# First layer of a four-layer network: input also channels first, norms moved to ScalarE, slots of some side work moved

## The chip, the cores and the metric

The kernel runs on one core of a Trainium2 chip. A core has five engines with a queue of instructions each: TensorE (PE in the profile, with its weight loads shown apart as PEld), VectorE (DVE), ScalarE (ACT), GpSimd (POOL) and SyncE (SP), which here issues the DMA transfers. The engines run side by side and wait for each other by semaphores; each takes its own instructions strictly in order. The metric is the device time of one execution in microseconds (us); lower is better. Times of one execution with the hardware profiler on give the trace.

## The reference, cut to what matters

Four layers follow each other on `x` of shape (4, 64, 64, 128). Only the first is touched. It is a two-dimensional selective-scan block with a group norm before it and a residual around it:

```
g   = group_norm(x)                                # 32 groups of 4 channels, per image
xh, z = split(g @ in_proj.T); z = silu(z)          # 256 channels each
xc  = silu(depthwise_conv3x3(xh) + conv_b)         # SAME padding
for k in 4 directions:                             # rows, columns, and both reversed
    dts, B, C = split(xs[k] @ x_proj[k])           # 8, 16 and 16 columns
    delta = softplus(dts @ dt_proj[k] + bias)
    h[t]  = exp(delta[t] * A) * h[t-1] + delta[t] * xs[t] * B[t]    # 16 states, 4096 steps
    y[k]  = sum over states of C[t] * h[t]  + D * xs
y   = layer_norm(y[0] + y[1] + y[2] + y[3])        # over 256 channels, per pixel
x   = x + (y * z) @ out_proj.T
```

The other three layers (a Fourier block, a neural-operator attention and a neighbourhood attention) read the result and are the same in both kernels.

## The kernel before, in words

`layer0` (from L83) goes through 128 *units*: 4 images x 4 directions x 8 chunks of 512 pixels (`units`, L512). A unit has 16 *slots*, one per state `n` of the scan, and a slot numbers the whole layer's time: `slot = 16 * i + n`. In text, "unit 5 of image 1" is the sixth unit of the second image.

In each slot: GpSimd multiplies `dB = du * B` for 1024 elements (L689); ScalarE makes two `dA = exp(delta * A)` (L694) into PSUM; VectorE runs two scans of 512 steps (L695); TensorE transposes 8 blocks of `h` from some slots earlier into the single PSUM tile `pt` (L542); ScalarE copies `pt` to `hT` (L552), which frees `pt`; TensorE multiplies the last slot's `hT` with the C weights into two `yT` banks (L577). Fixed extra steps lie in fixed slots by the table `TABLE`: the projection `x` in slot 6, its two copies in 7, and the delta steps between slots 7 and 12. The sum of a direction leaves the `yT` banks in slots 5 and 7 (L593).

The order on TensorE, ScalarE, VectorE and GpSimd is written out by hand (`tc.manual_schedule`). Work that does not belong to the scan is put between by *sides*: generators that yield one letter per piece, the kind of the piece. A kind may run only in the slots that `SIDE` lists, a piece keeps others off for `SPACE` slots, and `Side.due` spreads the pieces over the image. What a piece starts is finished by `later(place, f, slots=k)`: it is queued for `k` slots on, at a place in the slot (`dve` before the scans, `act0` after the first `dA`, `act1` after the second, `act2` after the copy `hT`). Two sides matter here:

- `before(b)` (L305) prepares image `b` while image `b - 1` is scanned. For each of 8 chunks it loads pixels-first input (`xs`, L313), transposes it on TensorE and takes statistics on VectorE (L318). After `group_scale` it loads the input again (`xt`), transposes it again (L336), and VectorE writes the scaled chunk from PSUM into the padded tile `xn` of 10 rows by 66 columns, with one or two more single rows for the neighbours (L635 with the tile `xn`). Then the two gate products `zp` (L177) with their SiLU, and two convolutions of nine taps each (L159), one tap in a slot, with theirs. SiLU is Exp, Ln, Exp on ScalarE and a product on VectorE (`silu`, L347).
- `after(b)` (L375) finishes image `b` while image `b + 1` is scanned: loads of `y` and `z`, aggregation, ln and exp for the factor `nb` (L396), the layer norm by VectorE (`normed`, L423, four instructions), transposes `pg` (L404), scale and shift on ScalarE into `yg`, the gating product on GpSimd (L412, kind `g`, only in slot 7 and only for images 0 to 2), the product with `w_out` (L417) in the PSUM tile `spare`, of which there is one, and the residual (L426). For image 3 it starts in that image's last quarter and takes each band as its last direction is done.

The first image's preparation (`opening`, L187) leaves two chunks' convolutions to a side `rest` (L297).

Of the kernel before, what the change touches and what calls it, by code (L numbers as in the profile page):

```python
# [17 lines left out]
P = 128  # L18
# [64 lines left out]
def layer0(sh, A, x_in, x_out, scr, ahead):  # L83
# [7 lines left out]
    with ExitStack() as ctx:  # L91
# [60 lines left out]
        def conv(xn, s, bank):  # L152

            for t in range(9):
                yield "c"
                if t == 0:
                    pm = bank("cv")
                dy, dx = divmod(t, 3)
                nc.tensor.matmul(  # L159
                    pm,  # L160
                    lhsT=taps[:, s, t, :],
                    rhs=xn[:, dy : dy + 8, dx : dx + 64],
                    start=(t == 0),
                    stop=(t == 8),
                )
            return pm
# [6 lines left out]
        def gates(b, c, v, bank, later, es=(None, None)):  # L173
            for s in range(2):
# [3 lines left out]
                silu(zp, 0.0, 0.0, scr(f"z{b % 3}")[s, :, c * CH : (c + 1) * CH], later, (("act1", 1), ("act2", 1), 2), es[s])  # L178
# [6 lines left out]
        def opening(bank, steps):  # L185
# [82 lines left out]
            for c in range(DENSE + 1):  # L268
# [9 lines left out]
                if c < DENSE:  # L278
                    for _ in gates(0, c, xg[:, 8 * c : 8 * c + 8], bank, soon):
                        pass  # L280
                    for _ in conv(xn, 0, lambda name: pm):
                        pass
# [15 lines left out]
        def rest(tiles, bank, later):  # L298

            for c, xn in enumerate(tiles, DENSE):  # L300
                for s in range(2):
                    pm = yield from conv(xn, s, bank)
                    grown(0, c, s, pm, later)

        def before(b, bank, later):  # L305
# [4 lines left out]
            for c in range(NCH):  # L310
                yield "l"
                t = tmp.tile([P, 4, DM], F32, name="xs", tag="t2", bufs=4)
                nc.sync.dma_start(t, tiles(x_in(b)[c * CH : (c + 1) * CH, :]))  # L313
                yield "m"
                pt = bank("gn_ps")
                for q in range(4):
                    nc.tensor.transpose(pt[:, q * P : (q + 1) * P], t[:, q, :], sh.ident)
                later("dve", lambda c=c, pt=pt: nc.vector.bn_stats(st[:, c, :], pt))  # L318
            yield "m"
            s_, o_ = sh.group_scale(st, psm, small, "m", exp_rstd)  # L320
            xn, ahead = None, rows()
            nc.gpsimd.memset(ahead[:, 0, :], 0.0)
            for c in range(NCH + 1):
                behind, xn = xn, ahead
                if c < NCH:
                    yield "l"
                    t = tmp.tile([P, 4, DM], F32, name="xt", tag="t2", bufs=4)
                    nc.sync.dma_start(t, tiles(x_in(b)[c * CH : (c + 1) * CH, :]))
                    if c < NCH - 1:
                        ahead = rows()  # L330
                    else:
                        nc.gpsimd.memset(xn[:, 9, :], 0.0)
                    yield "x"
                    pt = bank("x_ps")
                    for q in range(4):
                        nc.tensor.transpose(pt[:, q * P : (q + 1) * P], t[:, q, :], sh.ident)  # L336
                    grid = pt.rearrange("p (h w) -> p h w", w=64)
                    parts = [(xn[:, 1:9, 1:65], grid)]
                    if c > 0:
                        parts.append((behind[:, 9:10, 1:65], grid[:, 0:1]))  # L340
                    if c < NCH - 1:
                        parts.append((ahead[:, 0:1, 1:65], grid[:, 7:8]))
                    for dst, src in parts:
                        later("dve", nc.vector.tensor_scalar, dst, src, s_, o_, ALU.mult, ALU.add)
                    yield from gates(b, c, xn[:, 1:9, 1:65], bank, later)
                if c == 0:
                    continue  # L347
                for s in range(2):
                    pm = yield from conv(behind, s, bank)
                    grown(b, c - 1, s, pm, later)  # L350
# [24 lines left out]
        def after(b, st, later, bands):  # L375

            for c in bands:
# [15 lines left out]
                yield "n"  # L393

                nb = spare("nb")[:, 0:4]
                nc.scalar.activation(nb, rs, AF.Exp, scale=-0.5)  # L396
                for q in range(4):
                    later("dve", normed, y[:, q, :], mv[:, q, 0:1], nb[:, q : q + 1])
# [11 lines left out]
                if b < NB - 1:  # L410
                    yield "g"
                nc.gpsimd.tensor_tensor(yg, yg, z, ALU.mult)  # L412
                yield "m"
                op = spare("op").rearrange("p (q d) -> p q d", q=4)
# [140 lines left out]
        def products(G, q, hT):  # L555
# [67 lines left out]
            z={0, 1, 2, 3, 4, 11, 12, 13, 14, 15},  # L623
            c={11},
            g={7},
            f=(),
            l=(),
        )
        SPACE = dict(m=1, x=1, n=1, z=2, c=3, g=0)
# [11 lines left out]
        def flush_all():  # L641
            for at in range(slot, slot + 6):
# [3 lines left out]
        with tc.manual_schedule(engines=order):  # L646
# [3 lines left out]
            sides.append(Side(rest(left, spare, later), 18 * len(left), 0, 2 * NS * len(left)))  # L650
            for i, (b, k, c) in enumerate(units):
                if i % per == 0:
                    ln_st = small.tile([P, NJ, 1, 6], F32, name="ln_st")
                    first = len(left) if b == 0 else 0
                    if b + 1 < NB:
                        sides.insert(len(sides) if b == 0 else 0, Side(before(b + 1, spare, later), 17 + 8 * 22, NS * (i + first), (28 - first) * NS))
# [20 lines left out]
                for n in range(NS):  # L677
# [55 lines left out]
                    for d in inside or [d for d in sides if free and n in SIDE[d.need] and d.due(slot)][:1]:  # L733
# [3 lines left out]
                    for d in sides:  # L737
                        if d.need in ("f", "l") and d.due(slot):
# [38 lines left out]
class Side:  # L777


    def __init__(self, pieces, count, first, slots, loads=()):  # L780
        self.pieces, self.count, self.first, self.slots, self.loads = pieces, count, first, slots, list(loads)
        self.done, self.run, self.free_at = 0, 0, first
# [1298 lines left out]
def lay_out(i):  # L2081
# [96 lines left out]
    a["x"] = i["x"].reshape(4, NT, DM)  # L2178
    return {k: np.ascontiguousarray(v) for k, v in a.items()}
# [16 lines left out]
```

## Time and profile before

| | us |
|---|---|
| median of 3 runs (7655.22 to 7660.92) | 7658.74 |
| the profiled execution | 7655.2 |
| its span, first to last instruction | 7653.4 |
| scans of image 0 (111.9 to 1487.1) | 1375.2 |
| scans of image 1 (to 2871.1) | 1384.0 |
| scans of image 2 (to 4254.7) | 1383.6 |
| scans of image 3 (to 5611.5) | 1356.8 |
| the rest, mainly layers 1 to 3 | 2041.9 |

A line of a group in the profile names the line of the kernel, the engine, the operation, the tiles written and read, the shapes and the count; after the bar come the busy time, the mean duration in ns, and the idle time of the engine just before these instructions with what ended it. A line of a timeline has the start, the time from start to end of the merged instructions, the engine and the operation, and in brackets the wait before. An engine's instructions overlap a little at their ends, so the distance from start to start is some 0.09 us shorter than a duration. The helper `activation` and some others record a common line number, L635, so these are told apart by their tiles.

### The profile page before, as it was taken

How to read it: one execution, taken by the hardware profiler on the slowest of the kernel's cores; microseconds unless marked ns; L12 is line 12 of the kernel's file. 1: busy time of each engine (PE TensorE's matmuls, PEld its weight loads, DVE VectorE, ACT ScalarE, POOL GpSimd, SP SyncE). 2: the span in 40 equal slices, each digit the busy share in tenths (PEclk: the TensorE clock that was granted, in tenths of full speed). 3: DMA queues.
4: the chain of work that ended last, by engine and by line, in shares of the span. 5: the costliest groups of instructions: out<-in, count | busy, mean ns of one | idle time of the engine just before them, and what ended most of it. 6: DMA issues, size and time to landing. Idle time of an engine off the chain costs nothing.

```text
span 7653.4 us, 140855 instructions
## 1 busy us (share of the span) xinstructions
PE 6305.5 (82%) x52796; PEld 3991.3 (52%) x52796; DVE 6749.9 (88%) x8113; ACT 6088.5 (80%) x9683; POOL 5689.7 (74%) x2718
## 2 busy tenths in 40 slices
PE   7888888888889877888887777787789978686789
PEld 3544444444455544445554444454467756564556
DVE  7999999999999999999999999999966646656678
ACT  7999999999999999999999999999842323314667
POOL 4999999999999999999999999999920024123233
PEclk8999999999999999999999999999999979788999
DMA  5656566655666655565666445554533241231332
GB/s 171 179 172 176 179 174 175 172 171 170 192 178 179 188 187 177 158 187 179 179 186 189 168 170 180 180 184 170 185 99 73 57 113 54 77 105 43 103 99 80
DMA packets 1325854, 1158.86 MB, mean 151 GB/s; under 512 B 694133, under 2 KB 1119697, under 8 KB 1258226
## 3 DMA queue, kind: packets, MB, share of 16 engines
q1 hardware_dynamic: 1320898, 1147.43, 50.6%
q8 instruction: 416, 6.82, 0.4%
q10 hardware_dynamic: 4272, 2.43, 0.1%
q14 instruction: 268, 2.20, 0.1%
HBM read 956.37 MB, written 189.21 MB: 150 GB/s over the span
## 4 chain that ended last, share of the span: by engine, by line
ACT 35%; PE 33%; DVE 18%; issue 8%; POOL 3%; DMA 2%; SPq 1%; ACTq 0%; DVEq 0%; POOLq 0%
ACT hT L552 13%; ACT dA L694 13%; DVE h L695 11%; PE pt L542 6%; PE cv L159 5%; PE yT L577 3%; POOL dB L689 2%; ACT e L635 2%; PE pf L922 2%; PE po L935 1%; ACT delta L471 1%; PE pz L1166 1%; PE pt L1875 1%; ACT delta L474 1%; PE pu L1166 1%
## 5 line engine op out<-in xcount | busy, mean ns | idle before, releaser
L695 DVE TENSOR_TENSOR_SCAN h<-dA,state,dB 128x512 f32<-128x512 f32 x4096 | 4930.1, 1270 | 96.9 <-ACT dA L694 41.4
L689 POOL TENSOR_TENSOR dB<-du,Bb 128x1024 f32<-128x1024 f32 x2048 | 4813.5, 2389 | 153.4 <-DVE h L695 119.7
L542 PE MATMUL pt<-ident,h 128*128 128x128 f32 x16384 | 2215.0, 278 | 826.8 <-ACT hT L552 799.3
L694 ACT ACTIVATE dA<-delta,A_neg 128x512 f32<-128x512 f32 x4096 | 2752.8, 695 | 111.7 <-DVE h L695 91.2
L542 PEld LDWEIGHTS pt<-ident,h 128*128 128x128 f32 x16384 | 1806.9, 141 | 1862.5 <-ACT hT L552 1629.2
L552 ACT COPY hT<-pt 128x1024 f32<-128x1024 f32 x2048 | 2078.0, 1015 | 163.0 <-PE pt L542 143.1
L577 PE MATMUL yT<-hT,W 128*32 128x256 f32 x16384 | 1378.4, 409 | 0.4
L577 PEld LDWEIGHTS yT<-hT,W 128*32 128x32 f32 x16384 | 456.2, 151 | 342.0 <-issue 325.5
L159 PE MATMUL cv<-xn,taps 128*128 128x512 f32 x936 | 527.0, 644 | 2.5 <-DVE delta L477 2.5
L1166 POOL TENSOR_TENSOR xg<-xg,so 128x1024 f32<-128x1024 f32 x16 | 39.3, 2467 | 621.5 <-PE pu L1166 620.9
L1913 POOL TENSOR_TENSOR S<-S,sm 128x784 f32<-128x784 f32 x128 | 191.1, 1493 | 413.5 <-DVE sm L1911 239.6
L480 POOL TENSOR_TENSOR du<-delta,u 128x512 f32<-128x512 f32 x256 | 328.2, 1282 | 163.7 <-DVE delta L477 159.2
L468 PE MATMUL dp<-xd,w_dt 65*128 65x512 f32 x512 | 288.7, 646 | 40.3 <-DVE delta L477 29.4
L451 PE MATMUL yT<-u,w_x 128*48 128x512 f32 x508 | 245.3, 606 | 27.1 <-DVE y L593 26.5
L1920 ACT ACTIVATE S<-S,mx 128x196 f32<-128x196 f32 x512 | 227.9, 448 | 32.4 <-DVE mx L1947 31.8
L159 PEld LDWEIGHTS cv<-xn,taps 128*128 128x128 f32 x936 | 139.2, 188 | 179.9 <-issue 163.1
L923 ACT ACTIVATE h<-pf,b 128x512 f32<-128x512 f32 x128 | 87.6, 686 | 118.8 <-PE pf L922 100.8
L477 DVE SCALAR_TENSOR_TENSOR delta<-delta,dp 128x512 f32<-128x512 f32 x256 | 170.6, 667 | 2.5 <-ACT delta L474 1.0
L1166 POOL TENSOR_TENSOR WX<-wr,Xs 128x544 f32<-128x544 f32 x40 | 59.2, 1479 | 148.2 <-issue 63.2
L1875 PE MATMUL pt<-ident,S 128*98 128x128 f32 x1024 | 164.7, 285 | 3.4 <-POOL S L1913 2.0
L474 ACT ACTIVATE delta<-delta 128x512 f32<-128x512 f32 x256 | 164.6, 644 | 0.0
L471 ACT ACTIVATE delta<-dp 128x512 f32<-128x512 f32 x256 | 152.3, 595 | 11.7 <-PE dp L468 11.1
(381 smaller groups left out, 6937.3 us busy)
## 6 DMA issues: line engine op xcount, KB each, us to landing
Bb<-l_B SPq DMA_DIRECT2D x512, 1024.0 KB
W<-l_W SPq DMA_DIRECT2D x512, 256.0 KB
l_y<-y SPq DMA_DIRECT2D x127, 512.0 KB
u<-l_xr SPq DMA_DIRECT2D x64, 512.0 KB
u<-l_xw SPq DMA_DIRECT2D x64, 512.0 KB
y<-l_y SPq DMA_DIRECT2D x56, 512.0 KB
V<-l_v SPq DMA_DIRECT2D x512, 49.0 KB
y<-l_y SPq DMA_DIRECT2D x80, 256.0 KB
```

The costliest lines, as they stand in the source:

```text
L159: nc.tensor.matmul(pm, lhsT=taps[:, s, t, :], rhs=xn[:, dy : dy + 8, dx : dx + 64], start=(t == 0), stop=(t == 8),)
L451: nc.tensor.matmul(bank["x"], lhsT=w_x[:, s, k, :], rhs=u[:, s, :], start=(s == 0), stop=(s == 1))
L468: nc.tensor.matmul(bank[s], lhsT=w_dt[:, k, s * P : (s + 1) * P], rhs=xd, start=True, stop=True)
L480: nc.gpsimd.tensor_tensor(du[:, s, :], delta[:, s, :], u[:, s, :], ALU.mult)
L542: nc.tensor.transpose(pt[:, j, s, :], G["h"][:, s, t0 : t0 + 32, :].rearrange("p t n -> p (t n)"), sh.ident)
L552: return lambda: nc.scalar.copy(hT, pt.rearrange("p j s d -> p j (s d)"))
L577: nc.tensor.matmul(U["yT"][e][32 * jo : 32 * jo + 32, qo % 2, :], lhsT=U["Ws"][G["g"]][:, :, 4 * q + j], rhs=hT[:, j, :], start=((e, jo) n ...
L689: nc.gpsimd.tensor_tensor(dB, du, B_now[:, q : q + 1, :].to_broadcast([P, 2, CH]), ALU.mult)
L694: nc.scalar.activation(dA, delta[:, s, :], AF.Exp, scale=A_neg[:, k, s, n : n + 1])
L695: nc.vector.tensor_tensor_scan(h[:, s, :, q], dA, dB[:, s, :], state[:, s, n : n + 1], ALU.mult, ALU.add)
L1166: r = f(*args, **kw)
L1875: nc.tensor.transpose(pt[:, half, hp, :], U["S"][:, e, hp, 98 * half : 98 * half + 98], sh.ident)
```

## The change

The program gets a second copy of the input, `x_t`: channels first, with a border of zeros, 66 by 66 pixels.

- *Statistics.* `before` loads 8 rows of `x_t` per chunk into `xs`, and VectorE takes the statistics straight from it (new kind `s`). No transposes.
- *Scaling.* A chunk with its border rows is loaded whole into `xn` (at the first tap of the chunk before), and ScalarE scales it in place with one Identity activation, `scaled`, started at the sixth tap of the second convolution. No transposes, no work on VectorE, no zeros written by GpSimd.
- *Gates.* Kind `z` is bound to slots 13 and 1, and the three steps of its SiLU go into the following three slots instead of one.
- *Layer norm.* For images 0 and 1, VectorE makes a bias `mb` and ScalarE applies the norm with four Identity activations, one in each of four slots. The kind `t` runs in slots 11, 12, 15, 0, beside a convolution in progress.
- *Product with w_out.* For images 0 and 1 it runs in slot 8 (kind `o`), in the `yT` bank that the unit does not use yet.
- *Last image.* Its gating product is held to slot 7 for the bands 7 to 3.
- `before` starts in slot 0 of image 0, too, and its pace is 179 pieces in 27 units (193 in 28 before).

```diff
@@ before @@
-                t = tmp.tile([P, 4, DM], F32, name="xs", tag="t2", bufs=4)
-                nc.sync.dma_start(t, tiles(x_in(b)[c * CH : (c + 1) * CH, :]))
-                yield "m"
-                pt = bank("gn_ps")
-                for q in range(4):
-                    nc.tensor.transpose(pt[:, q * P : (q + 1) * P], t[:, q, :], sh.ident)
-                later("dve", lambda c=c, pt=pt: nc.vector.bn_stats(st[:, c, :], pt))
+                t = tmp.tile([P, CH], F32, name="xs", tag="t2", bufs=4)
+                nc.sync.dma_start(t.rearrange("p (h w) -> p h w", w=64), A["x_t"][b, :, 8 * c + 1 : 8 * c + 9, 1:65])
+                yield "s"
+                later("dve", nc.vector.bn_stats, st[:, c, :], t)
...
-                    yield "x"
-                    pt = bank("x_ps")
-                    for q in range(4):
-                        nc.tensor.transpose(pt[:, q * P : (q + 1) * P], t[:, q, :], sh.ident)
...
-                    for dst, src in parts:
-                        later("dve", nc.vector.tensor_scalar, dst, src, s_, o_, ALU.mult, ALU.add)
...
+            def load(c):
+                xn = tmp.tile([P, 10, 66], F32, name="xn", bufs=3)
+                nc.sync.dma_start(xn, A["x_t"][b, :, 8 * c : 8 * c + 10, :])
+                return xn
+
+            def scaled(xn, c, r0, r1):
+                inner = xn[:, max(r0, int(c == 0)) : min(r1, 10 - int(c == NCH - 1)), 1:65]
+                nc.scalar.activation(inner, inner, AF.Identity, scale=s_, bias=o_)
...
+                    for t, piece in enumerate(conv(xn, s, bank, out := [])):
+                        yield piece
+                        if c < NCH - 1 and (s, t) == (0, 0):
+                            ahead = load(c + 1)
+                        if c < NCH - 1 and s == 1 and t == 5:
+                            later("act2", scaled, ahead, c + 1, 0, 10)
@@ gates @@
-                silu(zp, 0.0, 0.0, ..., later, (("act1", 1), ("act2", 1), 2), es[s])
+                silu(zp, 0.0, 0.0, ..., later, (("act0", 2), ("act0", 3), 4), es[s])
@@ after @@
+                if b + 2 < NB:
+                    yield "t"
+                    nb = small.tile([P, 4], F32, name="nb")
+                    nc.scalar.activation(nb, rs, AF.Exp, scale=-0.5)
+                    mb = small.tile([P, 4], F32, name="mb")
+                    later("dve", nc.vector.scalar_tensor_tensor, mb, mv[:, :, 0], -1.0, nb, ALU.mult, ALU.mult, slots=2)
+                    for q in range(4):
+                        norm = dict(scale=nb[:, q : q + 1], bias=mb[:, q : q + 1])
+                        later("act2", nc.scalar.activation, y[:, q, :], y[:, q, :], AF.Identity, slots=2 + q, **norm)
...
-                if b < NB - 1:
+                if b < NB - 1 or c > 2:
                     yield "g"
                 nc.gpsimd.tensor_tensor(yg, yg, z, ALU.mult)
-                yield "m"
-                op = spare("op").rearrange("p (q d) -> p q d", q=4)
+                if b + 2 < NB:
+                    yield "o"
+                    op = psy.tile([P, 2, 2 * P], F32, name=f"yT{int(not rev)}").rearrange("p r d -> p (r d)")
+                else:
+                    yield "m"
+                    op = spare("op")
@@ the slots @@
-            z={0, 1, 2, 3, 4, 11, 12, 13, 14, 15},
+            z={13, 1},
+            s={11, 12, 13, 14, 15, 0, 1, 2, 3},
+            t={11, 12, 15, 0},
+            o={8},
...
-        SPACE = dict(m=1, x=1, n=1, z=2, c=3, g=0)
+        SPACE = dict(m=1, x=1, n=1, z=4, c=3, g=0)
...
+                        if d.need == "t" and n in SIDE["t"] and d.due(slot) and (inside or not any(o.taps for o in sides)):
+                            d.free_at = slot + 6
+                            d.step()
+                        if d.need == "o" and n in SIDE["o"] and d.due(slot - 8):
+                            d.step()
+                        if d.need == "s" and n in SIDE["s"] and d.due(slot):
+                            d.step()
@@ the host @@
+    a["x_t"] = np.pad(i["x"].reshape(4, 64, 64, DM).transpose(0, 3, 1, 2), ((0, 0), (0, 0), (1, 1), (1, 1)))
```

## The prediction

> **What bounds the kernel now.** I read the page first, then busy times by image, then single units, then timelines of two slots.
>
> ```profile
> PE 6305.5 (82%) x52796; PEld 3991.3 (52%) x52796; DVE 6749.9 (88%) x8113; ACT 6088.5 (80%) x9683; POOL 5689.7 (74%) x2718
> ```
>
> The change touches only the first layer, up to about 5630 us. Busy times of its four images (the columns after the stretch: its length, then PE, PEld, DVE, ACT, POOL busy, clock, DMA share, GB/s):
>
> ```profile
> 111.90:1487.10 1375.20, 1171.80 (x8928) 676.69 (x8928) 1341.17 (x1242) 1297.06 (x1861) 1277.64 (x589) 0.99 0.62 174
> 1487.10:2871.10 1384.00, 1171.65 (x9156) 689.79 (x9156) 1358.11 (x1316) 1304.17 (x1883) 1300.41 (x599) 1.00 0.61 180
> 2871.10:4254.70 1383.60, 1171.97 (x9156) 690.20 (x9156) 1357.79 (x1316) 1304.40 (x1883) 1300.29 (x599) 1.00 0.61 179
> 4254.70:5611.50 1356.80, 1043.03 (x8932) 644.79 (x8933) 1327.37 (x1309) 1253.49 (x1789) 1307.52 (x591) 0.99 0.51 175
> ```
>
> DVE is 97 to 98% busy, but ACT and POOL stand at 92 to 96%: freeing DVE gains only until the next engine. Single units (16 slots each): a bare one; one with nine taps and the end of one convolution; one in which the gating product follows well after the norms; one of the last seven of image 3.
>
> ```profile
> 5248.84:5288.83 39.99, 30.73 (x272) 18.31 (x264) 39.99 (x37) 38.48 (x55) 39.99 (x19) 1.00 0.49 170
> 1141.78:1184.10 42.32, 38.56 (x284) 21.48 (x283) 41.42 (x37) 40.63 (x59) 40.44 (x19) 1.00 0.47 128
> 2743.41:2787.38 43.97, 33.70 (x288) 21.02 (x288) 43.90 (x51) 40.23 (x59) 42.00 (x20) 1.00 0.77 252
> 5380.59:5426.83 46.24, 33.67 (x288) 21.05 (x288) 44.02 (x51) 40.01 (x59) 42.29 (x20) 1.00 0.54 183
> ```
>
> 40.0 us is the floor of DVE and POOL alike. From start-to-start distances without a wait: DVE 32 scans x 1.175 + 2 delta x 0.58 + 2 y x 0.58 = 39.9; POOL 16 dB x 2.335 + 2 du x 1.23 = 39.8; ACT 16 x (2 dA x 0.61 + hT 0.905 = 2.13) + 3.2 for delta, xd, Ct = 37.3. A slot with a tap is different (timeline of slots with taps):
>
> ```profile
> 1135.03 1.01 ACT L552 COPY hT<-pt 128x1024 f32<-128x1024 f32 x1 [0.31 <-PE pt L542]
> 1135.47 1.13 PE L159 MATMUL cv<-xn,taps 128*128 128x512 f32 x2
> 1135.94 1.31 ACT L694 ACTIVATE dA<-delta,A_neg 128x512 f32<-128x512 f32 x2
> ...
> 1136.43 1.04 PE L542 MATMUL pt<-ident,h 128*128 128x128 f32 x8
> 1137.40 0.67 PE L577 MATMUL yT<-hT,W 128*32 128x256 f32 x8
> 1137.56 1.01 ACT L552 COPY hT<-pt 128x1024 f32<-128x1024 f32 x1 [0.31 <-PE pt L542]
> ```
>
> hT to hT is 2.53 us: transposes, products and tap fill PE (0.97 + 0.60 + 0.96), and ACT waits 0.31 for it each time. DVE's need here is 2.35, so a tap slot costs 0.18 and has 0.4 us of ACT free. The work that is moved (DVE groups in the first layer):
>
> ```profile
> L423 DVE SCALAR_TENSOR_TENSOR yf<-yf,ln_mv,nb 128x256 f32<-128x256 f32 x124 | 50.6, 472 | 0.1
> ...
> L635 DVE TENSOR_SCALAR xn<-x_ps,gn_s,gn_o 128x512 f32<-128x512 f32 x24 | 19.0, 790 | 0.0
> ...
> L635 DVE TENSOR_SCALAR xn<-x_ps,gn_s,gn_o 128x64 f32<-128x64 f32 x42 | 12.7, 338 | 0.0
> ```
>
> And the gating at the end of a unit of image 3:
>
> ```profile
> 5419.72 2.36 POOL L412 TENSOR_TENSOR yg<-yg,zf 128x1024 f32<-128x1024 f32 x1 [1.75 <-ACT yg L635]
> 5422.04 4.72 POOL L689 TENSOR_TENSOR dB<-du,Bb 128x1024 f32<-128x1024 f32 x2
> 5424.45 2.46 DVE L695 TENSOR_TENSOR_SCAN h<-dA,state,dB 128x512 f32<-128x512 f32 x2 [2.15 <-POOL dB L689]
> ```
>
> POOL waited 1.75 for the gates' input, with the next dB queued behind, and DVE then waited 2.15.
>
> [...]the new statistics loads have 256 B pieces. The trace shows 27 ns for a 512 B packet and 11 for 64 B.
>
> **Prices.** The ACT norms have no row. [...]Estimates: layer norm, 256 elements, two pointers: 0.49 us; scaling, 640 elements: 0.81. Bounds: zero (all in ACT's free time) to the full 64 x 0.49 + 24 x 0.81 = 51 us.
>
> **The change, part by part.**
>
> *A. Gating in slot 7, image 3.* Units 25 to 31 now last 45.6, five times 46.2, 45.9: 322.5. With the gating in slot 7 POOL has some 4 us of lead, built by the norms (1.56), the y and statistics in slots 5 and 7. Units 27 to 30 then hold just what the 43.97 us unit holds, in the same slots. Unit 25 loses the gating (43.2), 26 the norms (42.4), 31 gets both (45.5): 43.2 + 42.4 + 4 x 44.0 + 45.5 = 307. Gain 15; between 10 and 17. The last band ends in the same slot, so the tail is unchanged.
>
> *B. Images 1 and 2, units 4 to 27.* Measured before: 1032 us, 43.0 a unit. After, a chunk takes three units exactly: gates in slots 13 and 1, a convolution from 11 to 3, another.
> First unit: the 42.3 kind, plus four aggregations 4 x 0.066 and the residual 0.57; the norms in slots 14, 15 make ACT 2.62 there against 2.38 and 2.40 measured: +0.5. The w_out product, 16 x 0.112 = 1.8 of PE in slot 8, spends ACT's lead that aggregation and residual give; it cost no DVE time in slot 11 before either. 43.6.
> Second unit: norm in slot 0 +0.1; in slot 1 a norm and the scaling meet: 0.905 + 0.49 + 0.81 + 1.22 = 3.43 against 2.53, +0.9; in slots 12 to 15 ACT has two yg (0.66), the column copy 0.93 and the first gate's Exp and Ln (0.48, 0.52): 4 x 2.13 + 3.25 = 11.8 against DVE's 9.4 and a lead of 0.4, +2.0. With 40.0 + 0.7 (four taps) + 1.1 (end of a convolution): 44.8.
> Third: two gate products on DVE 1.2, ACT remainder 0.2: 41.4.
> Sum 129.8, 43.3 a unit; over 24 units with the edges 1039: a loss of 7. DVE's 1.56 + 1.24 a chunk go, but DVE paid them outside tap slots, where they gave ACT its lead; now ACT pays in slots that PE fills.
>
> *C. Their units 0 to 3 and 28 to 31.* Before 178.1 and 173.6. Unit 1 loses four norms (43.6 to 41.8), unit 3 (46.0) the scaling, the x transposes and its bunched gates (to 40.7): 171. At the end no norms remain: 41.3 + 41.8 + 41.2 + 41.3 = 166. Gain 15. With B: 8 an image, 16 for both.
>
> *D. Image 0.* No layer norms. A chunk is 127.3 before (44.9 + 40.1 + 42.3). After: 42.3 + 43.2 (scaling in a tap slot +0.4, copy and gates in 13 to 15 +0.9) + 41.4 = 126.9. The first units, where statistics lie beside the left convolutions, and the last give 5 more. Gain 7.
>
> *At nothing.* The 192 PE transposes of x, 109 ns apart: PE is full only in tap slots, where none stood; in others DVE covers them. POOL memsets. SP: 48 loads before and after, in the same slots of the queue; 1024 packets of about 18 ns over 16 engines are 1.2 us against 0.9, 128 of 2640 B about 0.9. A statistics load is read four slots (9.6 us) after its issue; if it were late, DVE would stand with all scans behind it. The gates' SiLU over three slots is counted in B and D. Sixteen small products for the norm's bias fall into tap slots of DVE.
>
> Sum: -15 - 16 - 7 = -38. The profiled execution took 7655.2 (span 7653.4), 3.5 under the median: 7617 there, **7620 us** as median.
>
> **Rivals.** (1) *DVE is the bound throughout*: its relief 19.0 + 12.7 + 50.6 x 64/124 - 1 = 57, and 15 of A: 7587. For: 98% busy. Against: 0.31 waits in every tap slot and ACT at 94%. (2) *ACT takes all of it*: each norm costs 0.49 where I counted 0.1 to 0.25, 64 x 0.3 = 20, so images 0 to 2 give about nothing: 7642. For: pt has one buffer, so ACT's extra work delays the transposes too. Against: PE does the tap meanwhile. (3) *Slower, the product in slot 8*: PE already has x (1.8), d0 and d1 (0.96 each) in slots 6, 7 and 9, 11.8 us with the product against some 11.5 of DVE. If the product delays d1 and the residual, queued on DVE ahead of slot 10's scans, each may cost up to 3.5: 16 x 3.5 = 56, 7676. It decides from 2.4 us apiece. Against: bank and PE are free by my count. That pieces fall behind and are finished at an image's end without overlap I exclude: 179 pieces are due in 432 of 512 slots.
>
> **Numbers.** Own forecast 0.5 (7605 to 7632), rival 1 0.19, rival 2 0.21, rival 3 0.1. Range 7588 to 7652. No change is within 0.2%, 15 us, of 7658.7: a measurement hardly tells less. Rival 2 lies on that edge: half of it is "same". Faster 0.79, same 0.12, slower 0.09.
>
> **What would show it.** Image 3 near 1342, without DVE waits for dB above 1 us in its last units: A. Images 1, 2 near 1376: B and C; near 1360 is rival 1. ACT norms of 0.58 and scalings of 0.9 us: the prices. DVE idle for dA in slots 0, 1 and 12 to 15: B; idle in slots 8 to 10: rival 3. Any DVE wait of gn_st for a DMA would make me wrong.

## The result, and the profile after

The changed kernel takes 7645.06 us (median of 20 runs, 7640.59 to 7654.03) against 7657.40 (20 runs) for the kernel before on the same chip: a ratio of 0.9983, 95% interval 0.9977 to 0.9989, or 12 us less (8 to 18). The prediction was 7620, from a sum of -38. Sign and range held; the size was about a third of what I forecast.

Engines over the whole of the profiled execution (7645.85 us, span 7644.1), first part of the page:

```profile
PE 6293.8 (82%) x52604; PEld 3973.6 (52%) x52604; DVE 6715.7 (88%) x7999; ACT 6135.0 (80%) x9771; POOL 5691.9 (74%) x2688
```

DVE has 34 us less to do and ACT 47 us more: the work was moved as the change says. Busy times of the four images after (stretch, length, then PE, PEld, DVE, ACT, POOL busy, clock, DMA share, GB/s):

```profile
112.80:1480.70 1367.90, 1162.88 (x8864) 668.90 (x8864) 1330.54 (x1219) 1301.77 (x1869) 1277.32 (x579) 0.99 0.62 177
1480.70:2865.80 1385.10, 1167.87 (x9092) 682.99 (x9092) 1346.72 (x1270) 1325.07 (x1923) 1301.45 (x589) 1.00 0.61 181
2865.80:4249.00 1383.20, 1163.94 (x9092) 680.57 (x9092) 1346.76 (x1270) 1324.83 (x1923) 1301.45 (x589) 1.00 0.60 179
4249.00:5594.30 1345.30, 1043.66 (x8933) 644.93 (x8933) 1326.42 (x1309) 1253.20 (x1789) 1307.61 (x591) 0.99 0.52 176
```

| | before | after | difference | predicted |
|---|---|---|---|---|
| image 0 (D) | 1375.2 | 1367.9 | -7.3 | -7 |
| image 1 (B, C) | 1384.0 | 1385.1 | +1.1 | -8 |
| image 2 (B, C) | 1383.6 | 1383.2 | -0.4 | -8 |
| image 3 (A) | 1356.8 | 1345.3 | -11.5 | -15 |

With a start 0.9 later, the first layer ends 17.2 earlier (5594.3 against 5611.5). The pair of profiles shows only 9 us in all, because layers 1 to 3 took 8 us more in this execution. Their code is the same in every kernel here, and from the last scan of the first layer to the last instruction the profiles of all kernels below show between 2042 and 2055 us. The image times, which repeat within some 3 us from kernel to kernel where the code of an image is the same, carry the reading; the medians carry the total.

What became of DVE's relief in images 1 and 2 stands in the idle times of two groups. Groups of the kernel before in the stretch 1485 to 4250 (after the second bar: idle time of the engine just before them, and what ended it):

```profile
L695 DVE TENSOR_TENSOR_SCAN h<-dA,state,dB 128x512 f32<-128x512 f32 x2047 | 2470.2, 1270 | 41.9 <-ACT dA L694 25.9 <-issue 3.8 <-POOL dB L689 3.8
...
L552 ACT COPY hT<-pt 128x1024 f32<-128x1024 f32 x1024 | 1039.8, 1015 | 90.7 <-PE pt L542 81.7 <-ACT dA L694 0.3
```

The same groups after, in the same stretch:

```profile
L705 DVE TENSOR_TENSOR_SCAN h<-dA,state,dB 128x512 f32<-128x512 f32 x2046 | 2468.1, 1266 | 68.8 <-ACT dA L704 49.5 <-POOL dB L699 6.8 <-issue 4.5
...
L559 ACT COPY hT<-pt 128x1024 f32<-128x1024 f32 x1023 | 1040.4, 1017 | 52.0 <-PE pt L549 43.8 <-ACT dA L704 0.3
```

Over the two images DVE is busy for 22.4 us less (1358.11 + 1357.79 before, 1346.72 + 1346.76 after), and its scans wait 23.6 us more for dA (25.9 to 49.5). ACT is busy for 41.3 us more, and its copy waits 37.9 us less for TensorE's transposes (81.7 to 43.8). The moved work went into ACT's waits, as it should; but as much as DVE was spared came back as waits for ACT.

Counted by slots, from the first scan of one to the first scan of the next, the trade shows. In images 1 and 2 the 144 slots of each image in which TensorE runs a tap took 354.5 and 354.4 us before and 364.1 and 364.0 after; the other 368 took 1029.5 and 1029.2 before, 1021.0 and 1019.2 after. What was won in slots without a tap was lost in those with one. In image 0, beside which no layer norm runs, the 180 slots with a tap lost only 4.1 us (443.5 to 447.6) and the other 332 won 11.4 (931.7 to 920.3).

One thing the prediction had put at nothing. The group of the small product `mb` after, first layer:

```profile
L645 DVE SCALAR_TENSOR_TENSOR mb<-ln_mv,nb 128x4 f32<-128x4 f32 x16 | 22.9, 1428 | 0.0
```

`mb`, its "sixteen small products", takes 1.43 us for four elements: 22.9 us of DVE, nearly all of the 26.1 that the 64 norms on DVE had taken before in these images. A timeline of one (start, duration; DVE and POOL lines only):

```profile
1991.91 7.05 POOL L699 TENSOR_TENSOR dB<-du,Bb 128x1024 f32<-128x1024 f32 x3
1992.84 2.43 DVE L705 TENSOR_TENSOR_SCAN h<-dA,state,dB 128x512 f32<-128x512 f32 x2
1995.19 1.45 DVE L645 SCALAR_TENSOR_TENSOR mb<-ln_mv,nb 128x4 f32<-128x4 f32 x1
```

Instruction by instruction, each of the 16 ends 18 to 25 ns after a dB of GpSimd ends, however long before it began (1.2 to 2.0 us). So it waits inside the instruction, and no wait shows in the idle column.

Four line numbers in the text ahead of the prediction are off: `opening` begins at L185, `rest` at L298, `silu` at L352, and `units` is L503.

### The profile page after: what moved, and what is told of

The parts are those of the page before. It is cut to its first block, busy times and chain, and to the rows that moved or that the text cites. A ratio compares the mean times of both kernels' runs of the same rounds, so it can differ in the third digit from the quotient of the medians.

```text
span 7644.1 us, 140402 instructions
## 1 busy us (share of the span) xinstructions
PE 6293.8 (82%) x52604; PEld 3973.6 (52%) x52604; DVE 6715.7 (88%) x7999; ACT 6135.0 (80%) x9771; POOL 5691.9 (74%) x2688
## 4 chain that ended last, share of the span: by engine, by line
ACT 36%; PE 31%; DVE 18%; issue 8%; POOL 3%; DMA 2%; SPq 1%; ACTq 0%; DVEq 0%; POOLq 0%
ACT hT L559 14%; ACT dA L704 14%; DVE h L705 12%; PE pt L549 5%; PE cv L159 3%; POOL dB L699 3%; PE yT L584 3%; PE pf L939 2%; PE po L952 1%; ACT e L645 1%; ACT delta L478 1%; PE yT L458 1%; PE pz L1183 1%; PE pt L1892 1%; ACT delta L481 1%
```

## The experiments

Two explanations were open after these readings. The first, my theory ahead of the first run: VectorE is still the bound in images 1 and 2, and `mb` ate the gain. Its rival: ScalarE is the bound there, and what the change took from VectorE had been covered.

### The factor for the mean without its wait

```diff
-                    later("dve", nc.vector.scalar_tensor_tensor, mb, mv[:, :, 0], -1.0, nb, ALU.mult, ALU.mult, slots=2)
+                    for q in range(4):
+                        one = slice(q, q + 1)
+                        later("dve", nc.vector.tensor_scalar, mb[:, one], mv[:, q, 0:1], nb[:, one], -1.0, ALU.mult, ALU.mult, slots=2)
```

> The changed kernel, with the norm's bias mb made by four instructions that read one tensor from SBUF and a pointer scalar each, in place of one instruction that reads two tensors from SBUF. Theory (the one instruction of 1.43 us stood waiting for the end of the dB multiply that GpSimd had running[...]): the four take under 0.2 us each, 16 x (1.43 - 0.3) = 18 us of VectorE time go, part of it only moves ScalarE's lead: images 1 and 2 at 1375 to 1380 each against 1385.1 and 1383.2, the kernel 7 to 18 us below the changed one, 7627 to 7638. Rival (ScalarE is the bound there, so VectorE's wait is covered): mb gets short but images 1 and 2 stay within 2 us of 1385 and 1383, the kernel near 7645.

Measured: 7642.18 us (7637.35 to 7646.61), ratio to the kernel before 0.9978 (0.9969 to 0.9986). The tile `mb` in this kernel (duration in ns: least, median, most):

```profile
L647 DVE TENSOR_SCALAR mb<-ln_mv,nb x64: 183/204/208, 1691.3 to 4032.1; 128x1 f32<-128x1 f32 x64
```

The rival held and my theory did not. The wait is gone: DVE's busy time in images 1 and 2 falls from 1346.7 to 1342.0 each (the four parts still take some 0.55 us together). The images take 1384.3 and 1383.2: 0.8 and 0.0 less. So the wait was real and cost next to nothing: 9.5 us less of VectorE in the two images moved them by 0.8. That a scan which is held up lets ACT run ahead, so that the next slots are short, would explain it; no run tests that apart. DVE is not the bound in those slots. The later experiments on images 1 and 2 use this kernel as their base.

### What makes the small product slow

The kernel before, with one extra product of 128 by 4 elements in each chunk of the layer norm, whose result nothing uses. In the first kernel its second tensor `nb2` lies in SBUF, in the other it is `nb`, in PSUM. Both kernels also make `nb2`, with one more small Exp on ScalarE:

```diff
+                probe = small.tile([P, 4], F32, name="probe")
+                later("dve", nc.vector.scalar_tensor_tensor, probe, mv[:, :, 0], -1.0, nb2, ALU.mult, ALU.mult)
```
```diff
+                later("dve", nc.vector.scalar_tensor_tensor, probe, mv[:, :, 0], -1.0, nb, ALU.mult, ALU.mult)
```

> The kernel before with one unused small VectorE product per chunk of the layer norm (128x4, 32 in all), which reads two tensors from SBUF, and one more small Exp on ScalarE to make the second of them. [...]each product ends within 0.03 us of the end of a dB multiply and takes 1.2 us in the mean (0.1 to 2.4), 31 in the scanning part: 25 to 40 us slower than before. Rival (such a small product is slow in itself, or waits for ScalarE's factor): its time does not follow the ends of dB, and the next run, with the second tensor in PSUM, shows the same.

> The same unused small product, with its second tensor read from PSUM (the factor that the kernel before keeps there), and the same additional Exp. [...]0.16 us each whatever GpSimd does, the time 2 to 6 us above the one before. Rival: about 1.4 us each, as slow as the run with two SBUF tensors.

Measured: 7721.1 us (ratio 1.0084, 1.0069 to 1.0099) and 7661.52 (1.0003, 0.9995 to 1.0011). The probe with both tensors in SBUF (the profile leaves the 2 of `nb2` out):

```profile
L639 DVE SCALAR_TENSOR_TENSOR probe<-ln_mv,nb x32: 133/979/4558, 1534.2 to 5692.1; 128x4 f32<-128x4 f32 x32
```

and with the second in PSUM:

```profile
L639 DVE SCALAR_TENSOR_TENSOR probe<-ln_mv,nb x32: 129/132/159, 1533.6 to 5634.8; 128x4 f32<-128x4 f32 x32
```

Same operation, same place, same GpSimd work beside it; only the memory of one operand differs. With both tensors in SBUF, all 29 probes that met a dB end 17 to 27 ns after the end of one, and the three that met GpSimd idle took 0.13 to 0.16 us; with the second in PSUM, none of the 32 took more than 0.16. Why the one waits and the other does not, no run here shows. The whole became some 61 us slower, more than the 25 to 40 expected, and 50 of them lie in image 3, which took 1406.8 us. The timeline there:

```profile
4426.81 11.68 POOL L693 TENSOR_TENSOR dB<-du,Bb 128x1024 f32<-128x1024 f32 x5
4428.08 5.99 DVE L699 TENSOR_TENSOR_SCAN h<-dA,state,dB 128x512 f32<-128x512 f32 x5
4433.95 4.56 DVE L639 SCALAR_TENSOR_TENSOR probe<-ln_mv,nb 128x4 f32<-128x4 f32 x1
```

GpSimd runs dB after dB without a pause, and the probe, begun behind the start of the fourth, lasted to the end of the fifth (4.56 us). Five of the fifteen in image 3 lasted about 4.5 us, the longest of the others there 2.04. In images 1 and 2 the probes took 5.0 us each, and the images 4.6 and 4.0 more: in the kernel before, VectorE's time still counted there.

### Part A alone

The kernel before with one edit:

```diff
-                if b < NB - 1:
+                if b < NB - 1 or c > 2:
                     yield "g"
```

> The kernel before with the gating of the last image's bands 7 to 3 held to slot 7 and nothing else. Theory (parts are independent): image 3 goes from 1356.8 to about 1345.3, images 0 to 2 stay at 1375.2, 1384.0 and 1383.6 within 1 us, the kernel 11.5 us below the one before, about 7646. Rival (the gain is given back in the layers behind, as the profile of the changed kernel shows 8 us more there): the time within 4 us of the one before.

Measured: 7649.39 us, ratio 0.9988 (0.9981 to 0.9994); image 3 1344.9, the others 1375.1, 1385.2, 1383.0 as before. Part A is worth 11.9 us in the image times, alone as in the whole: most of what the change gains.

### Less and more work for ScalarE in images 1 and 2

Without the 64 norms on ScalarE, and with each done twice:

```diff
                     for q in range(4):
-                        norm = dict(scale=nb[:, q : q + 1], bias=mb[:, q : q + 1])
-                        later("act2", nc.scalar.activation, y[:, q, :], y[:, q, :], AF.Identity, slots=2 + q, **norm)
+                        pass
```
```diff
                         later("act2", nc.scalar.activation, y[:, q, :], y[:, q, :], AF.Identity, slots=2 + q, **norm)
+                        later("act2", nc.scalar.activation, y[:, q, :], y[:, q, :], AF.Identity, slots=2 + q, **norm)
```

> As the run with mb in four parts, without the 64 ScalarE activations that apply the layer norm for images 0 and 1 (these two images' layer norm is left out). Theory (in images 1 and 2 ScalarE is the bound around the taps, so what is moved to it costs time): images 1 and 2 fall from 1384.3 and 1383.2 to 1368 to 1376 each, that is 0.25 to 0.5 us for each norm of 0.49. Rival (VectorE is the bound, ScalarE has room): both stay within 2 us.

> As the run with mb in four parts, with each of the 64 norm activations made twice, one after the other, in the same slot (the layer norm of images 0 and 1 is applied twice). Theory of ScalarE as the bound: 32 x 0.49 = 15.7 us more on ScalarE in each of images 1 and 2, of which 11 to 16 show. Rival of room on ScalarE: 0 to 4 us each.

Measured: 7636.73 us (ratio 0.9971, 0.9960 to 0.9982) and 7689.52 (1.0039, 1.0025 to 1.0053). Images 1 and 2, one after the other. Without norms:

```profile
1480.40:2859.20 1378.80, 1165.28 (x9092) 683.20 (x9092) 1340.41 (x1294) 1310.99 (x1891) 1300.80 (x589) 1.00 0.62 181
2859.20:4238.70 1379.50, 1165.40 (x9092) 683.37 (x9092) 1340.35 (x1294) 1310.80 (x1891) 1300.55 (x589) 1.00 0.61 179
```

With norms twice:

```profile
1481.30:2886.00 1404.70, 1171.14 (x9093) 681.02 (x9092) 1342.10 (x1294) 1343.85 (x1955) 1301.51 (x589) 1.00 0.61 178
2886.00:4289.30 1403.30, 1170.19 (x9092) 680.38 (x9092) 1341.93 (x1294) 1343.88 (x1955) 1301.57 (x589) 1.00 0.60 176
```

Against the base (ACT busy 1324.5 and 1324.8): 38.5 us more of ACT in the two images cost 40.6, with DVE's busy time the same: 20 an image, more than the 11 to 16 expected. That is a bound. But 27.5 less gave only 9.1 (5.4 and 3.7), which lies between the two expectations. Where the other 18 went, the copy's group of the kernel without norms shows (1485 to 4250):

```profile
L560 ACT COPY hT<-pt 128x1024 f32<-128x1024 f32 x1027 | 1044.3, 1017 | 70.4 <-PE pt L550 62.4
```

The base has 44.3 there: ACT now waits 18.1 longer for the transposes. 9.1 + 18.1 is nearly all of the 27.5, and nearly all of the 18.1 lies in the slots with a tap: 34.5 us of such waits there in the base, 52.1 without the norms; 9.8 and 10.3 in the other slots. So two limits lie close together: take ACT's work away, and two thirds of it turn into waits for TensorE, whose single `pt` tile has to be filled behind the tap and the products. (No kernel here makes TensorE's part shorter, so this second limit is read from the waits and not tested.) And even with no layer norm on any engine these images are only 4 to 5 us shorter than before the change, short of the 8 that B and C were to give. Per norm, removing 64 gained 0.14 us and adding 64 cost 0.63.

### The scaling out of slot 1

```diff
-                        if c < NCH - 1 and s == 1 and t == 5:
+                        if c < NCH - 1 and s == 1 and t == 7:
                             later("act2", scaled, ahead, c + 1, 0, 10)
```

> The changed kernel with the factor for the mean in four parts, and the scaling of the next chunk two slots later (asked for at the eighth tap instead of the sixth, so in slot 3 and not in slot 1, where one of the norms meets it). If the meeting of the two costs what the prediction put there (0.9 us in slot 1, once in three units): 5 to 7 us less in each of images 1 and 2. If ScalarE is short over the whole stretch of slots 11 to 3, the work only changes its slot: 0 to 2 us less, or none.

Measured: 7647.93 us, ratio 0.9986 (0.9979 to 0.9992); images 1384.1 and 1383.2 against 1384.3 and 1383.2. The meeting of norm and scaling in slot 1 is in the trace (below), but moving it gains nothing in images 1 and 2: ACT is short over the stretch, not in that slot. Image 0, where no norm meets the scaling, even lost 4.8 us (1372.1 against 1367.3): its slots 1 became 5.5 us shorter in all, its slots 3 and 4 became 9.0 longer.

### The norms back on VectorE

First the layer norm of images 0 and 1; then the scaling with it:

```diff
-                        later("act2", nc.scalar.activation, y[:, q, :], y[:, q, :], AF.Identity, slots=2 + q, **norm)
+                        later("dve", nc.vector.tensor_scalar, y[:, q, :], y[:, q, :], nb[:, q : q + 1], mb[:, q : q + 1], ALU.mult, ALU.add, slots=2 + q)
```
```diff
-                nc.scalar.activation(inner, inner, AF.Identity, scale=s_, bias=o_)
+                nc.vector.tensor_scalar(inner, inner, s_, o_, ALU.mult, ALU.add)
```

> The changed kernel with the factor for the mean in four parts, and the 64 norms of images 0 and 1 back on VectorE, in the same slots 14, 15, 0 and 1 (or 1 to 4) as ScalarE had them: each reads one tensor and two pointers. If ScalarE is the bound in images 1 and 2 and VectorE has slack in the slots with taps: ScalarE's busy time there falls by some 18 us an image, VectorE's rises by 13 to 17, and the images take 1378 to 1384 (1384.3 and 1383.2 with the norms on ScalarE, 1378.8 and 1379.5 with no norms at all). If VectorE is the bound after all: 13 to 17 us more, 1397 to 1401 each.

> The changed kernel with both norms back on VectorE: the layer norms as in the run before it, and the 24 scalings of 640 elements as one multiplication with two pointers[...] in the slots where ScalarE had them. What is left of the change is the input channels first, the later SiLU, the product in slot 8 and the gating in slot 7. If ScalarE's free time is what is short: images 0 to 2 as with the layer norms alone on VectorE (1367.9, 1380.5, 1382.6) or 1 to 4 us less. If the scalings that VectorE was spared made image 0's gain: image 0 at 1373 to 1376, and images 1 and 2 some 6 us longer, 1386 to 1389.

Measured: 7641.28 us (ratio 0.9974, 0.9964 to 0.9985), images 1380.5 and 1382.6; and 7685.85 (1.0037, 1.0023 to 1.0050), images 0 to 2 1369.8, 1402.5, 1405.5. The layer norm may lie on either engine, as expected (1378 to 1384) if ScalarE is the bound: VectorE's busy time rose by 21.5 over the two images, its waits for dA fell from 57.0 to 35.8, and the time by 4.3. The scaling may not: both theories missed it, since most of its instructions last several times as long as the shortest. The group of its tile, from the kernel with both on VectorE:

```profile
L326 DVE TENSOR_SCALAR xn<-xn,gn_s,gn_o x24: 590/2653/4198, 332.8 to 3945.7; 128x640 f32<-128x640 f32 x18, 128x576 f32<-128x576 f32 x6
```

It has one tensor input and still waits for GpSimd: all but two of the 24 end 348 to 355 ns after the end of a dB. The two that took 590 ns had begun 0.24 us before the next dB, and it was that dB that took longer: 2.53 us, where the median is 2.38. Why an instruction with one tensor waits as the product with two does, no run here shows. The waits cost: the scalings take 18.2 and 20.6 us of VectorE in images 1 and 2, where eight of the shortest would be 4.7, and the images are 22 and 23 longer. In image 0, where they take 16.1, the image is only 1.9 longer. With more scaling on VectorE than the 10.6 us an image before the change, image 0 still keeps 5.4 of its 7.3 us. So image 0's gain does not come from VectorE's relief by the scaling; what makes it (the statistics without transposes, the gates' slots, or the copy of `x`) was not taken apart. And for images 1 and 2, what the moves would be worth without these waits stays open: no kernel here has a scaling on VectorE that reads SBUF without them. What is shown is that with the input read from SBUF, the scaling on VectorE is worse by 22 to 23 us in images 1 and 2, while the old one, read from PSUM, met no such wait (0.79 us in the mean for 512 elements, 0.80 at most).

### Taking other work from ScalarE

If ACT is the bound, its copies of columns (`by_columns`, 16 in each of images 1 and 2, with some 0.96 us each from start to start and 1.20 from start to end) are the thing to move. GpSimd takes them, first in slot 9; in the second kernel the gating of bands 2 and 1 of the last image is also held to slots 4 and 15; in the third the copy is one slot later, in slot 10; in the fourth the scaling lies in slot 3 as well. (In the diff, `slots=6` becomes 7 from the third on, and the new kind `h` may run in slots 4 and 15.)

```diff
-            later("act0", gather or by_columns, xo, scr(f"xw{b % 2}")[s], c, slots=10)
+            if gather:
+                later("act0", gather, xo, scr(f"xw{b % 2}")[s], c, slots=10)
+            else:
+                later("pool", by_columns, xo, scr(f"xw{b % 2}")[s], c, slots=6)
...
-            nc.scalar.copy(xw.rearrange("p w h -> p h w"), xo.rearrange("p (h w) -> p h w", w=64))
+            nc.gpsimd.tensor_copy(xw.rearrange("p w h -> p h w"), xo.rearrange("p (h w) -> p h w", w=64))
...
+                elif c > 0:
+                    yield "h"
```

> As the run with mb in four parts, with the 52 column copies xw (L362, 0.93 us of ScalarE each) made by GpSimd in slot 9 in place of slot 13. Theory of ScalarE as the bound: 14.9 us of ScalarE go in each image, in clumped slots 12 to 15, where ScalarE is behind: images 1 and 2 at 1370 to 1377, image 0 at 1359 to 1365; [...]the kernel at 7610 to 7625. Rival (GpSimd, at 94 percent, becomes the bound): images 0 to 2 within 3 us of where they were or above.

> As the run before this, with the gating products of bands 2 and 1 of the last image held to slots 4 and 15. Theory (GpSimd stood waiting for ScalarE's yg with the next dB behind it, twice in unit 31 of image 3): that unit falls from 47.4 to 43 to 45 us, image 3 to 1341 to 1343, the rest as in the run before. Rival (the w_out product of band 1 comes after the last scan and lengthens the tail): image 3 as said, but the end of layer 0 no earlier.

> As the run with the copies on GpSimd and the last unit relieved, but each copy one slot later, in slot 10, so that its transfer no longer stands ahead of the row of broadcasts on SyncE's queue. If that order made the one slot of 7.3 to 7.9 us in each of images 0 to 2: those slots are gone, images 1 and 2 at 1371 to 1375, image 0 at 1357 to 1361, and the whole near 7617. If the cause is another (the transfer's time itself, or GpSimd busy with copies): images 1 and 2 stay at 1377 to 1382 and the whole near 7636.

> The previous kernel (copies on GpSimd in slot 10) with the scaling in slot 3 too. With the copies gone from ScalarE it has spare time in slot 3: 1 to 4 us less in each of images 1 and 2 than with the copies alone, if the meeting in slot 1 still costs; no difference above 1 us if GpSimd (16 products a unit and now the copies) has become the bound.

| | median | ratio to before, 95% | image 0 | 1 | 2 | 3 |
|---|---|---|---|---|---|---|
| copy in slot 9 | 7634.18 | 0.9967 (0.9955 to 0.9980) | 1365.1 | 1379.1 | 1379.7 | 1345.1 |
| and last unit | 7637.82 | 0.9970 (0.9959 to 0.9981) | 1365.3 | 1379.8 | 1379.4 | 1341.1 |
| copy in slot 10 | 7622.56 | 0.9953 (0.9941 to 0.9966) | 1362.6 | 1374.8 | 1375.8 | 1342.9 |
| and scaling in slot 3 | 7625.96 | 0.9956 (0.9943 to 0.9968) | 1367.0 | 1374.6 | 1375.8 | 1341.6 |

With the copy in slot 9, images 1 and 2 stayed above the 1370 to 1377 expected and the whole above 7625, and the copy takes 1.15 us of GpSimd. The relief of the last unit shows in image 3 (4 us) and not in that run's median, whose interval holds such a difference either way. With the copy in slot 9 the periods fell, but one slot in each of images 0 to 2 lasted over 7 us. One such slot, after the copy of 2487.64 on GpSimd (SP lines; the durations are those of its queue entries):

```profile
2488.82 0.58 SPq L366 DMA_DIRECT2D l_xw<-xw  x1
2489.49 4.54 SPq L467 DMA_DIRECT2D l_B<-xd  x1
...
2497.16 0.34 SPq L503 DMA_DIRECT2D Bb<-l_B  x1
```

The copy's transfer stands on SP's queue ahead of the store and the broadcast of B, so that the next unit's Bb came late and GpSimd stood for it (its idle time that ended with a Bb's arrival is 29.8 us in this kernel, 11.9 in the one with slot 10 and 7.4 in the kernel before). In slot 10 it comes behind them, and the same stretch reads:

```profile
2483.33 0.37 SPq L469 DMA_DIRECT2D l_B<-xd  x1
...
2486.34 0.44 SPq L505 DMA_DIRECT2D Bb<-l_B  x1
...
2492.42 0.58 SPq L366 DMA_DIRECT2D l_xw<-xw  x1
```

Bb is issued 3.0 us after the store of B (2483.33 to 2486.34) and not 7.7 after it (2489.49 to 2497.16), the unit with the long slot takes 43.9, and the kernel is the best of this study: 36 us under the kernel before (26 to 45), where my forecast for the change had been 38. The long slots are gone, as expected; the times came out a little above the expectation (7617 for the whole, 1371 to 1375 for images 1 and 2). Most of what it gains beyond the changed kernel it gains where the theory says: images 1 and 2 are 10 and 7 us shorter than after the change, images 0 and 3 are 5 and 2. Its scans (1485 to 4250):

```profile
L713 DVE TENSOR_TENSOR_SCAN h<-dA,state,dB 128x512 f32<-128x512 f32 x2058 | 2481.8, 1267 | 65.5 <-ACT dA L712 31.4 <-POOL dB L707 16.6 <-issue 10.2
```

Waits for dA are 25.6 lower than in the base (57.0), those for dB 11.2 higher (5.4 there): GpSimd is the next engine by these waits. The scaling in slot 3 added nothing here either, in images 1 and 2, and lengthened image 0 by 4.4.

Last, this best kernel with the layer norm on VectorE:

> The kernel with the column copies on GpSimd in slot 10, with the 64 layer norms of images 0 and 1 on VectorE. If ScalarE still bounds images 1 and 2 once the copies are gone from it: 1 to 4 us less in each (below 1374.8 and 1375.8), the whole 7614 to 7621. If VectorE has become the bound there: 3 to 13 us more in each, the whole 7628 to 7650.

Measured: 7640.63 us, ratio 0.9978 (0.9971 to 0.9985), images 1382.8 and 1385.8: 8 and 10 more. The norm's group says why (1485 to 4250):

```profile
L652 DVE TENSOR_SCALAR yf<-yf,nb,mb 128x256 f32<-128x256 f32 x64 | 50.2, 784 | 0.0
```

The same norm takes 0.38 us where it does not wait; in 64 of them 26 us are waits for GpSimd, 14 more than before the copies (36.0 us in all there): 18 of the 64 last 1.4 to 2.4 us, and all of these end 146 to 155 ns after an instruction of GpSimd. So once ACT is relieved, VectorE with such waits is the bound. The norms belong on ScalarE then, and the copies do not.

## Why the prediction was right or wrong

**A, gating in slot 7: right in kind, -11.5 for -15.** Units 27 to 30 take 44.0 each, as counted. The rest was mis-sized in two units. Unit 26 I gave 42.4, since it "loses the norms"; it keeps four of them, in slot 15, and takes 43.9. Unit 31 I gave 45.5; it takes 47.9, longer than before (45.9). Bands 2 to 0 are not held to a slot, and their products stand in POOL's queue ahead of dB. After the change, in unit 31:

```profile
5550.97 2.36 POOL L414 TENSOR_TENSOR yg<-yg,zf 128x1024 f32<-128x1024 f32 x1 [2.71 <-ACT yg L645]
```

At 5587.07 it waits for the next one's input again, 3.52 us. With bands 2 and 1 held to slots 4 and 15, unit 31 took 43.7.

**B, units 4 to 27: the period right, its edges not.** In image 1 the period of three units is 129.5 to 130.4 for the 129.8 counted, in units 4 to 6 and 10 to 24; the 24 units take 1043.5 for 1039. Of the 4.5 over, 1.3 lie in units 7 to 9 (131.1) and 2.6 in units 25 to 27 (132.4), where unit 27 took 44.0 for the 41.4 of the third unit of a period; the cause of these is open. The slot that I priced at 3.43, where norm and scaling meet, lasts 3.45 from one copy hT to the next. In its ACT timeline:

```profile
1875.18 0.60 ACT L645 ACTIVATE yf<-yf,mb,nb 128x256 f32<-128x256 f32 x1
1875.68 0.92 ACT L326 ACTIVATE xn<-xn,gn_o,gn_s 128x640 f32<-128x640 f32 x1
1876.50 1.28 ACT L704 ACTIVATE dA<-delta,A_neg 128x512 f32<-128x512 f32 x2
```

From start to start 0.50 and 0.82, where the prediction had 0.49 and 0.81; the full durations 0.60 and 0.92 for 0.58 and 0.9. The prices ahead of the runs were estimates of mine with no line of the profile before behind them; this trace is what supports them. Of the 49.5 us that scans of images 1 and 2 wait for dA, 14.0 stand before the scans of slot 2, behind that meeting in slot 1, and 22.8 in slots 13 to 15 (8.9 before the change): near what "what would show it" says, but in slots 0 and 1 themselves only 0.7. The rest, in slots 5 and 6, fell from 16.8 to 11.5.

**C, units 0 to 3 and 28 to 31: the step that failed,** together with B's edges. C was to save 15 us in each of images 1 and 2, and B to cost 7. C saved 10.2 and 11.6, B cost 11.2 and 11.3, and nothing is left of the 16 us of both images. Against the 171 + 166 counted for C, image 1 shows 174.0 + 167.6 and image 2 173.1 + 166.8. Unit 3 is the clearest: "from 46.0 to 40.7" counts what VectorE loses. Unit 3 of image 1, before and after (columns as for the images):

```profile
1619.23:1665.27 46.04, 36.07 (x289) 20.92 (x291) 44.67 (x45) 44.63 (x68) 42.71 (x21) 1.00 0.53 177
1611.24:1654.69 43.45, 32.32 (x270) 18.98 (x269) 40.88 (x37) 41.80 (x62) 38.48 (x18) 1.00 0.40 134
```

VectorE's work is what I had counted, 40.9 us. But the unit takes 43.5: ScalarE, with the first scaling and six steps of the gates (twelve before), is itself busy for 41.8, and VectorE waits 1.7 us for its dA, in slots 2, 3 and 6. Around the convolutions I had priced ACT; here I took VectorE's relief as time. Why units 28 and 29 of image 1 stand 1.1 and 0.3 above the count was not taken apart.

**D, image 0: -7.3 for -7,** and its period 41.6 + 42.3 + 43.0 = 126.9 as counted in sum (42.3 + 43.2 + 41.4). The reason I gave for the part outside the period (statistics beside the left convolutions) is not tested apart.

**At nothing.** `mb` was wrong as a price (1.43 us each instead of some 0.06) and right as a cost: removing its wait changed images 1 and 2 by under 1 us. SP's loads, the transposes and the memsets give no wait that I found: the statistics `gn_st` from `xs` never wait for a DMA.

**Prices.** Without the norms on ACT, its copy waits 62.4 us for the single `pt` tile to be filled, against 44.3 in the base. Whether a second `pt` would take these waits away was not tried. The statistics took 675 ns in the mean from PSUM before and 667 from SBUF after. The packets of 256 B took 18 ns in the median, as estimated.

**Rivals.** Rival 2, *ACT takes all of it*, at 7642, lands 3 us from the result. Its sum is what happened in images 1 and 2, but its reason is not shown: it put 0.49 us on each norm, and taking the norms away gained 0.14 each, within the 0.1 to 0.25 that I had counted. So most of what is missing there is not the layer norm's; how much the scaling and the new slots of the gates take was not separated. For image 0 rival 2 was wrong. I had set against it that TensorE does the tap meanwhile; that wait of ACT's was indeed spent (37.9 of 41.3 us), and still nothing was left over. Rival 1 (7587) falls with the first experiment. Rival 3 falls by the trace: with the product, slots 8 to 10 of a unit last 9.11 us (3.22, 2.95, 2.95) against 8.25 (2.95, 2.37, 2.93) without, and the difference is VectorE's own work, the residual with 0.57 and the four aggregations with 0.27; no scan waits there for ACT.

Image 3 near 1342 came to 1345, images 1 and 2 near 1376 to 1385 and 1383: of the 38 us, 18 are there in the image times and 12 in the medians.

## What to carry to other kernels

When work moves from one nearly full engine to another, count both at every stretch, the edges too: an engine's relief is time only where the other engines have slack, and here 22 us of it became 24 us of waits for the engine that took the work. Test the new bound from both sides: here adding work cost in full, while removing it gained only up to the next limit. And before moving a transfer's source to another engine, read the order of the DMA queue behind it: here one slot decided between 7638 and 7623 us.

## What the runs showed of the hardware

- The small product on VectorE with both tensors in SBUF, four elements per partition, took 0.28 to 4.56 us beside a busy GpSimd and 0.13 to 0.16 where GpSimd was idle; with one of them in PSUM, 0.13 to 0.16 throughout. Where it waited, it ended 17 to 27 ns after the end of a dB of GpSimd, and in image 3 five of fifteen lasted about 4.5 us, nearly two dB of 2.38 each.
- The scaling and the layer norm on VectorE (a multiplication and addition with two pointers and one tensor, from SBUF to SBUF) waited in the same way. The scaling, mostly of 640 elements, took 0.59 us in the two cases where it began before a dB, and 2.65 in the median of all 24; 22 of them ended 348 to 355 ns after the end of a dB. In the two cases of 0.59 us the dB took 2.53 us for 2.38. The norm, of 256 elements, took 0.38 where it did not wait; in the kernel with the copies in slot 10, 18 of 64 took 1.4 to 2.4 and ended 146 to 155 ns after an instruction of GpSimd.
- These waits lay inside the instructions' durations: they raised VectorE's busy time (22.9 us for the 16 `mb`, 50.2 for those 64 norms) and left the idle column at 0.0. The sign of them was a mean duration that did not fit the size of the tile: 1.43 us for four elements.
